# The last unit of the last cross-attention in a four-layer decoder gets its own PSUM layout

## The chip, the cores and the metric

The kernel runs on one core of a Trainium2 chip. The time is device microseconds of one launch, the median of three runs. Each profile is one execution, recorded by the hardware profiler, with its own time. Engines are written as in the profile: PE is TensorE's matmul, PEld its weight load, DVE VectorE, ACT ScalarE, POOL GpSimd, SP SyncE (which issues most DMAs). L263 means line 263 of the kernel.

## The reference, cut to what matters

A token stream x of 1024 positions and 128 channels passes four decoder layers, each with a self-attention, a cross-attention over a context of 6404 positions, and a feed-forward part. The change lies in the cross-attention of the last layer, which has 16 heads of 8 channels and a mask over the context:

```
q = _split_heads(Q @ Wq.T + bq)
k = _split_heads(K @ Wk.T + bk)
v = _split_heads(V @ Wv.T + bv)
scores = jnp.einsum('bhqd,bhkd->bhqk', q, k) / np.sqrt(D_HEAD).astype(np.float32)
scores = jnp.where(mask == 0, jnp.float32(-1000000000.0), scores)
attn = jax.nn.softmax(scores, axis=-1)
ctx = jnp.einsum('bhqk,bhkd->bhqd', attn, v)
...
return ctx @ Wo.T + bo
```

After it comes the last feed-forward part, a mixture of eight experts, and then the result is written.

## The kernel before, in words

**Tiling.** `l3_xattn` handles the 16 heads in four groups `g` of four heads, and the 1024 queries in two halves `h` of 512. One combination is a unit, `n = 2 * g + h`, so there are eight. In a unit, `pairs_core` loops over the context in 51 tiles of 128 keys (the last one has 4). The rows of two heads lie together in one tile of 128 partitions, 64 rows per head: the query and the key are split into bf16 parts stacked along these rows, and further rows carry the mask and the negative of each query's maximum. A matmul over the 64 rows thus gives scores that already have the maximum taken off, and the exponential needs nothing else. Such a two-head tile is called a pair; a unit has two pairs, `kP[0]`, `kP[1]` and `qP[0]`, `qP[1]`.

**One key tile of a unit.** For each of the four heads there is one score matmul (128 keys by 512 queries, one PSUM bank), one exponential from PSUM to SBUF, and one matmul with the values. The values have nine columns, the ninth all ones, so the sum of the exponentials comes with the result. The four heads' results go to four strips of 32 partitions in one bank, `acc`. The values of a tile are issued after the scores of the next tile (the list `late`), so that the PE need not wait for exponentials just started.

**Two forms of the loop.** `pairs_core` has two forms, chosen by whether the caller passes a list of work to do beside it:

```
        wide = beside is None
        matmul = nc.tensor.matmul if wide else self.matmul
...
                if wide:
                    both = ps.tile([P, 2, BANK], F32, tag="s", name="s")
                    p2 = pool.tile([P, 2, BANK], F32, tag="p", name="p", bufs=5)
...
                else:
                    ss = [ps.tile([P, BANK], F32, tag="s", name="s") for _ in range(2)]
                    pp = [pool.tile([P, BANK], F32, tag="p", name="p", bufs=10) for _ in range(2)]
...
                if wide:
                    nc.scalar.activation(p2[:n], both[:n], func)
                else:
                    for j in range(2):
                        nc.scalar.activation(pp[j][:n, :w], ss[j][:n, :w], func)
```

In the wide form a pair's scores lie in two neighbouring banks and one activation covers both heads (L1353); the matmuls show as L1348 (scores) and L1327 (values). In the narrow form each head has its own bank and activation (L1356), and all matmuls go through the helper at L263, which keeps them in the order of the program. The second layer's cross-attention, `l2_xattn`, uses the wide form in all eight units, with a sigmoid, 48 rows and eight value columns; its PSUM layout is one bank `m`, three pairs of banks `s` and one bank `acc`.

**What stands beside the units.** Each unit of `l3_xattn` but the last does the maxima of the next unit beside its own loop: `maxima(n + 1)` gives `pairs_max`, whose score matmuls go to pairs of banks `m2`, and VectorE reduces them (L1284). At its end `pairs_neg` negates the maxima, splits them into three bf16 parts in `mpad`, transposes them on the PE (L1304), and adds them into the next unit's `qP` on VectorE (L1306, once per pair). The last unit gets an empty tuple, so nothing stands beside it, but it is still the narrow form. The PSUM of all eight units is two `m2` pairs (four banks), three banks `s` and one bank `acc`.

**After the loop.** VectorE or ScalarE, by turns, copies `acc` to SBUF as `oT` (L269, L271). `pairs_norm` transposes it on the PE (L1377), takes the reciprocal of the sums (L1380) and writes the scaled result into `o` (L1382). After the eighth unit VectorE adds the value bias (L1725), and the output projection and the experts follow.

**Order.** Each engine has one queue that it works through in order. A scheduler puts the instructions in the queues by data and buffer dependences; a tile waits until the earlier user of its buffer is through, and a new pool's tile until earlier users of the same memory are.

Of the kernel before, what the change touches and what calls it, by code (L numbers as in the profile page):

```python
# [10 lines left out]
F32 = mybir.dt.float32  # L11
# [3 lines left out]
AF = mybir.ActivationFunctionType  # L15
ALU = mybir.AluOpType
AX = mybir.AxisListType
PSUM = bass.MemoryType.PSUM

P = 128  # L20
# [5 lines left out]
BANK = 512  # L26
# [188 lines left out]
class Decoder:  # L215
# [1156 lines left out]
    def pairs_norm(self, ps, pool, oT, o, g, h):  # L1372

        nc = self.nc
        m = ps.tile([P, 2, BANK], F32, tag="m2", name="m2")[:, 0, :]
        for i in range(4):
            nc.tensor.transpose(m[:, i * P:(i + 1) * P], oT[:, i * P:(i + 1) * P], self.ident)  # L1377
        mv = m.rearrange("p (t j r) -> p t j r", t=4, r=32)
        rd = pool.tile([P, 4, 4], F32, tag="rd", name="rd")
        nc.vector.reciprocal(rd, mv[:, :, :, 8])  # L1380
        ov = o[:, 4 * h:4 * h + 4, 32 * g:32 * g + 32].rearrange("p t (j r) -> p t j r", r=8)
        nc.vector.tensor_tensor(ov, mv[:, :, :, 0:8], rd[:, :, :, None].to_broadcast([P, 4, 4, 8]), ALU.mult)  # L1382
# [290 lines left out]
    def l3_xattn(self):  # L1673
        nc, tc = self.nc, self.tc
        w, some, kd = self.w3, self.some, self.kd3
        wo, bq = w[:, 384:512], w[:, 512:513]
        bv, bo = w[:, 514:642], w[:, 642:770]
        qd = self.dram.tile([P, 8, S], BF16, name="qd3")
        with tc.tile_pool(name="x", bufs=2) as pool:
            v = pool.tile([P, NKT, 16, 9], F32, tag="v", name="v", bufs=1)  # L1680
            nc.gpsimd.memset(v[:, :, :, 8:9], 1.0)
            mpad = pool.tile([P, 2, 4, P], F32, tag="mpad", name="mpad", bufs=1)
            nc.gpsimd.memset(mpad, 0.0)
            o = pool.tile([P, NT, D], F32, tag="o", name="o", bufs=1)
            kPs = [self.kP0, [pool.tile([P, NK], BF16, tag=f"kP{k}", name="kP", bufs=1) for k in range(2)]]
            qPs = [[pool.tile([P, S], BF16, tag=f"qP{i}{k}", name="qP", bufs=1) for k in range(2)] for i in range(4)]
            with tc.tile_pool(name="x0", bufs=2) as pool0, tc.tile_pool(name="x0_ps", bufs=2, space=PSUM) as ps0:
                ps = _Psum(ps0, m=2, m2=3)
                for i, src in ((6, some[:, 1:2]), (7, self.eps[:, 2:3])):
                    f = pool0.tile([P, BANK], BF16, tag="bar", name="fill")  # L1690
                    nc.vector.tensor_copy(f, src.to_broadcast([P, BANK]))
                    for h in range(2):
                        nc.sync.dma_start(out=qd[:, i, h * BANK:(h + 1) * BANK], in_=f)
                self.layernorm(ps)
                self.add_bias(bo)
                for _, hs, m in self.hidden(ps, [w[:, :128]], [self.xT]):
                    q = pool0.tile([P, BANK], F32, tag="k", name="q")
                    nc.vector.tensor_scalar(q, m, bq, some[:, 0:1], ALU.add, ALU.mult)
                    self.split(pool0, q, qd, self.QPART, hs.start, hs.stop)
                for g in range(4):  # L1700
                    self.pairs_read(qPs[g], qd, g, S)
                self.pairs_read(kPs[1], kd, 1, NK)
                vs = self.all_values(ps, v, w[:, 256:384], nc.scalar.copy)
                for step in self.pairs_max(ps, pool0, qPs[0], kPs[0], 0, mpad):
                    step(0)
                    step(1)
                    next(vs, None)
            with tc.tile_pool(name="x1", bufs=2) as pool1, tc.tile_pool(name="x1_ps", bufs=2, space=PSUM) as ps0:
                ps = _Psum(ps0, m2=2, s=3, acc=1)

                def maxima(n):
                    if n < 8:
                        return self.pairs_max(ps, pool1, qPs[n // 2], kPs[n // 2 % 2], n % 2, mpad)
                    return ()

                for n in range(8):
                    g, h = n // 2, n % 2
                    oT = pool1.tile([P, BANK], F32, tag="oT", name="oT")
                    self.pairs_core(ps, pool1, qPs[g], kPs[g % 2], v, g, h, oT, AF.Exp, 64, maxima(n + 1))
                    if h == 1 and g < 2:  # L1720
                        self.pairs_read(kPs[g], kd, g + 2, NK)
                    self.pairs_norm(ps, pool1, oT, o, g, h)
            with tc.tile_pool(name="x2", bufs=2) as pool2, tc.tile_pool(name="x2_ps", bufs=2, space=PSUM) as ps0:

                nc.vector.tensor_tensor(o, o, bv[:, None, :].to_broadcast([P, NT, D]), ALU.add)  # L1725
                self.small_out(_Psum(ps0, m=8), pool2, o, wo)
        self.held.close()
# [92 lines left out]
```

## Time and profile before

| | us |
|---|---|
| median of 3 runs | 6397.46 (6395.14 to 6400.81) |
| profiled execution, its own time | 6402.34 |
| its span, first to last instruction | 6400.5 |
| PE busy | 5934.1 (93%) |
| DVE busy | 3537.8 (55%) |
| ACT busy | 2987.7 (47%) |
| POOL busy | 2230.2 (35%) |

The units of the last cross-attention lie between about 5185 and 6207 us of the span. The last one begins with its first score matmul at 6086.04 and ends with the copy of `oT` at 6207.12; the experts end with the span at 6400.5. In the stretch from 6082 to 6207 the PE is busy for 100.16 us, ACT for 105.15, DVE for 2.77 and POOL not at all; DMA is near zero.

A row of instructions in time gives start, length, engine, line, operation, output and inputs, shape and how many were merged; in brackets stand the idle time before it and what ended that. A row of a group gives busy time and mean duration, and after the bar the idle time of its engine before these instructions. Durations of neighbours overlap in a pipeline, so the step from start to start is shorter than a duration.

### The profile page before, as it was taken

To read this page: it belongs to the slowest core of one execution; us is meant where nothing else is said; L and a number is where in the kernel's file an instruction comes from. 1 tells how busy PE (TensorE), PEld (TensorE's weight loads), DVE (VectorE), ACT (ScalarE), POOL (GpSimd) and SP (SyncE) were. 2 spreads that over 40 slices of the span, in tenths; PEclk is the share of its full clock that TensorE was granted. 3 is DMA by queue.
4 is the path that set the end of the run, shared out by engine and by line. 5 is a ranking of instruction groups with operands and counts; after the bars stand their busy time and mean duration, and the time that the engine had idled before them with its cause. 6 is when DMAs were issued, how large, how long until landed. Compare 5 with 4: busy or idle time off the path is not lost. (4 is left out here: it accounts for less than half of the span.)

```text
span 6400.5 us, 78103 instructions
## 1 busy us (share of the span) xinstructions
PE 5934.1 (93%) x30090; PEld 2158.5 (34%) x30090; DVE 3537.8 (55%) x6777; ACT 2987.7 (47%) x4024; POOL 2230.2 (35%) x1074
## 2 busy tenths in 40 slices
PE   6799999999999999999899968999988679999979
PEld 2233333434343434333375432111133211211126
DVE  5476666666666666664235461100025799999913
ACT  2323333343433333334311226999920058888872
POOL 1036667677676667678331530100001000000000
PEclk7799999999999999999989978999998679999999
DMA  3000000000000000000000013200023100000000
GB/s 102 4 1 1 1 1 1 1 1 1 1 1 1 1 1 1 1 6 7 31 2 14 0 67 92 66 16 1 1 80 103 52 1 21 1 21 1 1 6 29
DMA packets 65196, 118.23 MB, mean 18 GB/s; under 512 B 10510, under 2 KB 46630, under 8 KB 62774
## 3 DMA queue, kind: packets, MB, share of 16 engines
q1 hardware_dynamic: 64246, 109.95, 5.4%
q8 instruction: 236, 3.87, 0.2%
q10 hardware_dynamic: 576, 3.28, 0.2%
q14 instruction: 138, 1.13, 0.1%
HBM read 81.74 MB, written 31.41 MB: 18 GB/s over the span
## 5 line engine op out<-in xcount | busy, mean ns | idle before, releaser
L759 POOL TENSOR_TENSOR tot<-tot,p 128x1024 f32<-128x1024 f32 (+1 forms) x800 | 1885.2, 2357 | 668.4 <-ACT p L751 635.3
L678 DVE CUSTOM_DVE_ANT_0 junk<-m,bars 128x512 f32<-128x512 f32 (+1 forms) x1664 | 1114.4, 670 | 617.9 <-PE m L675 489.9
L751 ACT ACTIVATE p<-s,drop,keep 128x1024 f32<-128x1024 f32 (+1 forms) x416 | 500.7, 1204 | 1489.3 <-PE s L744 1475.7
L1284 DVE TENSOR_REDUCE mx<-m 128x2 f32<-128x1024 f32 (+4 forms) x928 | 1026.9, 1157 | 91.0 <-PE m L263 80.3
L1356 ACT ACTIVATE p<-s 128x512 f32<-128x512 f32 (+3 forms) x1824 | 924.7, 591 | 266.7 <-PE s L263 266.0
L675 PE MATMUL m<-kT,qT 64*128 64x512 f32 (+1 forms) x3328 | 940.9, 607 | 1.2 <-DVE mx L678 0.8
L739 PE MATMUL s<-qT,kT 64*128 64x512 f32 (+1 forms) x3264 | 832.5, 599 | 9.5 <-DVE p L749 9.5
L726 PE MATMUL acc<-p,v 128*64 128x512 f32 (+1 forms) x3264 | 791.2, 605 | 0.8 <-ACT p L751 0.7
L1353 ACT ACTIVATE p<-s 128x1024 f32<-128x1024 f32 (+1 forms) x816 | 750.9, 1179 | 27.3 <-PE s L1348 27.3
L749 DVE TENSOR_TENSOR p<-s,every 128x1024 f32<-128x1024 f32 x400 | 489.8, 1224 | 196.6 <-PE s L739 113.1
L1327 PE MATMUL acc<-p,v 128*8 128x512 f32 (+1 forms) x3264 | 552.4, 598 | 0.0
L751 ACT ACTIVATE p<-p,drop,keep 128x1024 f32<-128x1024 f32 x400 | 492.5, 1231 | 44.4 <-DVE p L749 44.0
L263 PE MATMUL m<-kP,qP 64*128 64x512 bf16 (+4 forms) x1856 | 374.0, 399 | 118.1 <-DVE mx L1284 57.5
L263 PE MATMUL acc<-p,v 128*9 128x512 f32 (+3 forms) x3648 | 471.5, 589 | 0.0
L739 PEld LDWEIGHTS s<-qT,kT 64*128 64x128 f32 (+1 forms) x3264 | 332.8, 187 | 395.7 <-issue 340.9
L675 PEld LDWEIGHTS m<-kT,qT 64*128 64x128 f32 x3328 | 305.5, 186 | 475.2 <-DVE mx L678 227.3
L263 PE MATMUL s<-qP,kP 64*128 64x512 bf16 (+3 forms) x1824 | 431.8, 385 | 33.2 <-ACT p L1356 29.8
L726 PEld LDWEIGHTS acc<-p,v 128*64 128x64 f32 (+1 forms) x3264 | 197.0, 136 | 530.3 <-issue 527.4
L1348 PE MATMUL s<-qP,kP 48*128 48x512 bf16 (+1 forms) x1632 | 250.9, 386 | 1.6 <-ACT p L1353 1.6
L269 DVE COPY oT<-acc 128x512 f32<-128x512 f32 x16 | 11.0, 689 | 431.6 <-PE acc L1327 301.8
L263 PEld LDWEIGHTS <-qP 64*128 64x128 bf16 x1856 | 122.9, 96 | 337.0 <-issue 263.4
L263 PEld LDWEIGHTS <-kP 64*128 64x128 bf16 x1824 | 94.1, 94 | 398.0 <-issue 390.0
(454 smaller groups left out, 4954.8 us busy)
## 6 DMA issues: line engine op xcount, KB each, us to landing
kd<-part SPq DMA_DIRECT2D x156, 128.0 KB
wb<-expert_weights SPq DMA_DIRECT2D x30, 512.0 KB
kP<-kd SPq DMA_DIRECT2D x24, 512.0 KB
kP<-kd SPq DMA_DIRECT2D x48, 192.0 KB
w_expert<-in_Y_w SPq DMA_DIRECT2D x8, 768.0 KB
qd<-part SPq DMA_DIRECT2D x36, 128.0 KB
qP<-qd SPq DMA_DIRECT2D x16, 256.0 KB
w_decay<-in_c_decay SPq DMA_DIRECT2D x4, 1024.0 KB
```

The lines of the kernel that those rows point to most:

```text
L263: return self.tc.keep_in_program_order(self.nc.tensor.matmul(*a, **k))
L675: nc.tensor.matmul(m[:, :b - a], lhsT=qT[r, q0:q0 + P], rhs=kT[r, a:b], start=True, stop=True)
L678: nc.vector.tensor_tensor_reduce(junk[:, :b - a], m[:, :b - a], bars[:, a:b], 1.0, -3.0e38, ALU.add, ALU.max, mx[:, t, j, c:c + 1])
L726: nc.tensor.matmul(acc[64 * j:64 * j + 64, :], lhsT=v[:n, t, 64 * j:64 * j + 64], rhs=pr[:n, j, :], start=t == 0, stop=t == NKT - 1, tile_ ...
L739: nc.tensor.matmul(s[:n, j, :], lhsT=kT[r, t * P:t * P + n], rhs=qT[r, hs], start=True, stop=t > t0)
L749: nc.vector.tensor_tensor(pr[:n], s[:n], every[:n], ALU.add)
L751: nc.scalar.activation(pr[:n], s[:n], AF.Exp, bias=drop[:n, t:t + 1], scale=keep[:n, t:t + 1])
L759: nc.gpsimd.tensor_tensor(tot[:n], tot[:n], pr[:n], ALU.add)
L1284: nc.vector.tensor_reduce(mx[:, t, 2 * pair:2 * pair + 2, c:c + 1], m[:, :, :b - a], AX.X, ALU.max)
L1327: matmul(acc[32 * j:32 * j + v.shape[3], off:], lhsT=v[:n, t, 4 * g + j, :], rhs=ws[j][:n, :BANK - off], start=t == 0, stop=t == nkt - 1, ...
L1353: nc.scalar.activation(p2[:n], both[:n], func)
L1356: nc.scalar.activation(pp[j][:n, :w], ss[j][:n, :w], func)
```

## The change: one more block for the last unit

The loop over units now ends after the seventh. The eighth runs in pools of its own, with the PSUM layout of the second layer's cross-attention: one bank `m`, three pairs of banks `s`, one bank `acc`. It is called without a list of work beside it, so that `pairs_core` takes the wide form. `pairs_norm` takes a bank `m` where the pool has no `m2`.

```diff
     def pairs_norm(self, ps, pool, oT, o, g, h):
 
         nc = self.nc
-        m = ps.tile([P, 2, BANK], F32, tag="m2", name="m2")[:, 0, :]
+        m = ps.tile([P, 2, BANK], F32, tag="m2", name="m2")[:, 0, :] if "m2" in ps.bufs else self.m(ps)
         for i in range(4):
             nc.tensor.transpose(m[:, i * P:(i + 1) * P], oT[:, i * P:(i + 1) * P], self.ident)
...
-                for n in range(8):
+                for n in range(7):
                     g, h = n // 2, n % 2
                     oT = pool1.tile([P, BANK], F32, tag="oT", name="oT")
                     self.pairs_core(ps, pool1, qPs[g], kPs[g % 2], v, g, h, oT, AF.Exp, 64, maxima(n + 1))
                     if h == 1 and g < 2:
                         self.pairs_read(kPs[g], kd, g + 2, NK)
                     self.pairs_norm(ps, pool1, oT, o, g, h)
+
+            with tc.tile_pool(name="x3", bufs=2) as pool1, tc.tile_pool(name="x3_ps", bufs=2, space=PSUM) as ps0:
+                ps = _Psum(ps0, m=1, s=3, acc=1)
+                oT = pool1.tile([P, BANK], F32, tag="oT", name="oT")
+                self.pairs_core(ps, pool1, qPs[3], kPs[1], v, 3, 1, oT, AF.Exp, 64)
+                self.pairs_norm(ps, pool1, oT, o, 3, 1)
             with tc.tile_pool(name="x2", bufs=2) as pool2, tc.tile_pool(name="x2_ps", bufs=2, space=PSUM) as ps0:
```

## The prediction

> **What bounds the kernel now.** I read the order of instructions in time around the last unit first, since only that unit is edited; then its groups with their idle time; then the same loop in the second layer's cross-attention, which already has the layout that the unit gets; then the granted clock in narrow stretches.
>
> One key tile of the last unit in the kernel before, in order of time (start, us, engine, line, operation):
>
> ```profile
> 6132.98 0.60 PE L263 MATMUL s<-qP,kP 64*128 64x512 bf16 x3
> 6133.41 2.06 ACT L1356 ACTIVATE p<-s 128x512 f32<-128x512 f32 x4 [0.29 <-PE s L263]
> 6134.06 0.37 PE L263 MATMUL s<-qP,kP 64*128 64x512 bf16 x1 [0.47 <-ACT p L1356]
> 6134.36 0.12 PEld L263 LDWEIGHTS acc<-p,v 128*9 128x9 f32 x8 [1.09 <-issue]
> 6134.36 1.05 PE L263 MATMUL acc<-p,v 128*9 128x512 f32 x8
> ```
>
> Three score banks are filled, the fourth score matmul waits until ScalarE has read the first of them, the values of the tile before (`acc`) are queued behind that fourth matmul on the in-order TensorE, and the next tile's scores are queued behind the values. So ScalarE runs dry once per tile: 0.29 us. Two such ACT rows start 2.353 us apart (6133.41 to 6135.76, 6138.12). Groups of the same stretch (6082 to 6206), busy and mean, then the idle time before:
>
> ```profile
> L1356 ACT ACTIVATE p<-s 128x512 f32<-128x512 f32 x200 | 103.1, 604 | 20.8 <-PE s L263 20.8
> L263 PE MATMUL acc<-p,v 128*9 128x512 f32 x400 | 52.3, 595 | 0.0
> L263 PE MATMUL s<-qP,kP 64*128 64x512 bf16 x200 | 49.7, 383 | 23.3 <-ACT p L1356 22.5 <-DVE qP L1306 0.2
> ```
>
> Each engine waits for the other: 20.8 us on ScalarE, 23.3 us on TensorE. VectorE, busy in all earlier units with the maxima of the next unit, has none to take here, and the stages after wait for this unit, so its length is path. Now the same loop in pairs of banks, one period in the second layer's cross-attention (48 rows and a sigmoid in place of 64 rows and an exponential):
>
> ```profile
> 4240.98 0.60 PE L1348 MATMUL s<-qP,kP 48*128 48x512 bf16 x4
> 4241.51 0.10 PEld L1327 LDWEIGHTS acc<-p,v 128*8 128x8 f32 x4 [0.42 <-issue]
> 4241.51 1.36 PE L1327 MATMUL acc<-p,v 128*8 128x512 f32 x8
> 4241.85 0.10 PEld L1327 LDWEIGHTS acc<-p,v 128*8 128x8 f32 x4 [0.23 <-ACT p L1353]
> 4242.81 0.11 PEld L1348 LDWEIGHTS <-kP 48*128 48x128 bf16 x4 [0.86 <-issue]
> ```
>
> The next period's scores are at 4242.81: 1.83 us. No score waits; the second half of the values waits 0.23 us for ScalarE, so ScalarE sets the pace. ScalarE's own rows, of that stage's last unit and of the start and end of the unit that is changed:
>
> ```profile
> 4585.55 93.36 ACT L1353 ACTIVATE p<-s 128x1024 f32<-128x1024 f32 x102
> ...
> 6086.74 4.03 ACT L1356 ACTIVATE p<-s 128x512 f32<-128x512 f32 x8 [6.94 <-PE s L263]
> ...
> 6203.99 2.02 ACT L1356 ACTIVATE p<-s 4x512 f32<-4x512 f32 x4 [0.27 <-PE s L263]
> ```
>
> 102 double-width activations in one piece with no idle time: 93.36 us. The same 51 key tiles take 119.27 us in the changed unit (6086.74 to 6203.99 + 2.02 = 6206.01).
>
> **The change, part by part.**
>
> *Width of the exponentials.* 204 of 512 become 102 of 1024. Step from one 512 to the next without a wait: (2.06 - 0.60) / 3 = 0.487 us. Of 1024: (93.36 - 1.0) / 101 = 0.914 us. A pair costs 0.974 now and 0.914 then: 102 x 0.060 = 6.1 us.
>
> *Layout.* Six banks of scores instead of three. In the new order of TensorE one more tile's scores stand in PSUM while ScalarE works, so the wait per tile goes: 2.353 - 4 x 0.487 = 0.405 us per tile (0.29 idle, the rest lost overlap), about 49 times 0.405 = 19.8 us (first two tiles already run without it). Sum of both: 25.9, and the end-to-end figures give the same: 119.27 - 93.36 = 25.9 us.
>
> The wide row is a sigmoid's. From both sides: 0.914 as in that row (gain 25.9), or no gain from the width at all, two narrow steps, 0.974 (99.4 us, gain 19.9). I take the row: the same line, shape, memory spaces and engine, and the narrow exponential and the wide sigmoid fit one line: 0.914 - 0.487 = 0.427 us for 512 more elements, which leaves 0.060 per instruction. [...]
>
> *Rows and columns.* 64 rows for 48 and 9 value columns for 8 change no time: 383 ns mean against 386 for scores, 595 against 604 for values. TensorE's work per tile is 0.53 for scores and 1.05 for values, 1.58 us, under 1.83.
>
> *The seam.* New pools open between units 7 and 8. In the built order TensorE's queue is the same there (mpad transposes, oT transposes, mpad transposes, eight scores, four values), but the first score now lies in banks of the last `m2` tile and waits for VectorE's second addition into qP. Before, it started at 6086.04; that addition ends at 6086.15 + 0.69 = 6086.84, so the score starts at 6086.89. Behind it on TensorE stand only this unit's scores. The first exponential then needs two matmuls: 0.49 us after the first score at full clock in the second layer (4105.33 to 4105.82), 0.60 at 4584.95 with ScalarE busy; I take 0.55, which gives 6087.44 instead of 6086.74: +0.7 us. `acc` is cleared after that addition instead of at 6080.85: 0.48 us on an idle VectorE, ended near 6087.4, a microsecond before the first values; uncovered it would be 0.48. No DMA and no other queue's order changes; SP's and GpSimd's lists are the same but for line numbers.
>
> *The norm.* One bank named `m` instead of half of `m2`; its transposes wait for the copy of `oT` as before. The last exponential to that copy was 1.11 us (6206.01 to 6207.12), and 1.12 in the second layer (4678.91 to 4680.03). Nothing.
>
> Sum: -25.9 + 0.7 = -25.2 us. The profiled execution was 6402.34 with a span of 6400.5; its span becomes 6375.3. It lies 4.9 above the median of the runs shown, all of which have the same unit, so the median goes from 6397.46 to **6372.3 us**.
>
> *What the shift meets.* After the unit come 193 us of output projection and experts, TensorE at work nearly throughout, with the clock at half in two stretches. Narrow stretches of the profile, the granted clock the number after POOL's:
>
> ```profile
> 6080.00:6085.00 5.00, 1.88 (x9) 1.58 (x9) 3.35 (x13) 0.00 (x0) 0.00 (x0) 0.53 0.00 0
> 6085.00:6090.00 5.00, 4.25 (x17) 1.42 (x20) 1.24 (x3) 3.26 (x7) 0.00 (x0) 0.79 0.02 3
> ...
> 6210.00:6215.00 5.00, 4.45 (x20) 4.21 (x21) 1.62 (x3) 1.87 (x2) 0.00 (x0) 0.50 0.02 1
> ...
> 6225.00:6230.00 5.00, 5.00 (x13) 3.05 (x12) 2.46 (x11) 0.60 (x1) 0.00 (x0) 0.50 0.34 118
> 6230.00:6235.00 5.00, 5.00 (x12) 2.10 (x12) 2.59 (x13) 4.25 (x6) 0.00 (x0) 0.95 0.10 39
> ```
>
> [...] I take 0 and put +-3 in the range. [...]
>
> **The rivals.**
>
> *The unit keeps a wait.* If three pairs are too few and ScalarE still loses its 0.29 us on every tile: 51 x 0.29 = 14.8 back, gain 10.4, 6387. For it: three pairs are still less than two tiles of scores. Against: the second layer's unit of 102 without a gap has the same three pairs.
>
> *The exponential is slower wide than the sigmoid.* Up to the upper bound, gain 19.2, 6378; nothing in the trace asks for it.
>
> [...]
>
> *No change.* The edit would have to miss the path. VectorE's idle 120 us before the copy of `oT` and the next stage's start right after it speak against; and the built kernel does contain 102 wide exponentials there.
>
> **How the numbers follow.** As worked out, with the tail's and seam's few microseconds: 0.86. Wide exponential slower or two clock windows lost (6378 to 6382): 0.05. A wait kept (about 6387): 0.04. No change: 0.02. Slower: 0.03. Likeliest 6372.3; its own range is -25.9 and 3 better in the tail, 6368.5, to 19.2 gained, 6378.3. The range for 8 in 10 is 6367.5 to 6379. What a measurement can tell from no change is 0.2%, 12.8 us, so faster is 0.86 + 0.05 and, where the kept wait is shorter, 0.01: 0.92; same 0.05 (the rest of the kept wait and no change); slower 0.03.
>
> **What would show it.** Right: the groups have L1353 of 102 (100 and two of 4 rows) between about 6087.4 and 6180.8 in one piece, idle time of it near zero; scores 1.83 us apart; the copy of `oT` at about 6182; the first wide score waiting for the addition into qP. Wrong: a row "PE s" with waits for ACT on every tile, starts 2 us or more apart, the exponentials' step above 0.95, or a clock under 1.00 in the middle of the unit. [...]

## The result

| | before | after |
|---|---|---|
| median, us | 6397.46 (7 executions, 6390.38 to 6425.81) | 6371.28 (7 executions, 6361.88 to 6381.14) |
| profiled execution, its own time | 6402.34 | 6379.08 |
| its span | 6400.5 | 6377.3 |
| second addition into qP ends, to copy of `oT` | 120.28 | 95.06 |
| exponentials of the unit, first start to last end | 119.27 | 93.41 |
| copy of `oT` to the end of the span | 193.38 | 193.19 |

The ratio of after to before is 0.9957, with a 95% interval of 0.994 to 0.9975: faster, by 26 us as the medians stand. The forecast was 6372.3, a difference of 25.2.

In the two profiles the difference of the spans is 23.2 us, and it can be split at the unit's edges. The stretch from the end of the second addition into qP to the copy of `oT` is 25.22 shorter; the tail after it is 0.19 shorter; and the changed kernel reached that addition 2.21 us later (6089.05 against 6086.84), in work that the change does not touch. 25.22 + 0.19 - 2.21 = 23.2. Executions of either kernel spread over 19 us and more, and the spread goes with the granted clock of the whole execution (in the rounds below the kernel before took 6379.13 us at a mean clock of 0.943 and 6425.13 at 0.933). The stretch from the addition to the copy repeats far better: 95.06 and 96.07 in two profiles of the change. The experiments below are therefore compared by this stretch, and by whole times only where there were rounds.

One key tile of the changed unit, in order of time (start, us, engine, line, operation):

```profile
6134.76 0.60 PE L1348 MATMUL s<-qP,kP 64*128 64x512 bf16 x4
6135.29 0.10 PEld L1327 LDWEIGHTS acc<-p,v 128*9 128x9 f32 x4 [0.42 <-issue]
6135.29 1.36 PE L1327 MATMUL acc<-p,v 128*9 128x512 f32 x8
6135.62 0.10 PEld L1327 LDWEIGHTS acc<-p,v 128*9 128x9 f32 x4 [0.23 <-ACT p L1353]
6136.59 0.11 PEld L1348 LDWEIGHTS <-kP 64*128 64x128 bf16 x4 [0.86 <-issue]
```

The next tile's scores start at 6136.59, 1.83 us on, where it was 2.353. The four scores run without a wait; what waits is the second half of the values, 0.23 us, for an exponential. The period is the second layer's to the hundredth, with 64 rows instead of 48 and an exponential instead of a sigmoid.

The groups of the changed stretch (6080 to 6185), busy and mean, then the idle time before:

```profile
L1353 ACT ACTIVATE p<-s 128x1024 f32<-128x1024 f32 x100 | 91.8, 1196 | 7.1 <-PE s L1348 7.1
L1327 PE MATMUL acc<-p,v 128*9 128x512 f32 x400 | 68.6, 595 | 0.0
L1348 PE MATMUL s<-qP,kP 64*128 64x512 bf16 x200 | 30.3, 381 | 1.5 <-DVE qP L1306 0.8 <-ACT p L1353 0.7
```

The 22.5 us that TensorE waited for ScalarE are gone but for 0.7. The 7.1 us that ScalarE still waits stand before the first exponential, where the maxima are finished. They stood there before, too, and are part of the 20.8 us in the group's row of the kernel before, as its waits show (total, times, longest):

```profile
ACT p L1356 <- PE s L263: 21.1, 50, 6.9
```

The longest wait, 6.9 us, is the one before the first exponential. So what is gone is the waits within the loop, about 14 us, and with them the overlap of neighbouring exponentials that each of them broke. ScalarE's own row of the changed unit:

```profile
6089.58 93.41 ACT L1353 ACTIVATE p<-s 128x1024 f32<-128x1024 f32 x102 [7.15 <-PE s L1348]
```

All 102 in one piece: a step of (93.41 - 1.0) / 101 = 0.915 us. The seam (the place where the seventh unit ends and the eighth begins), the engines together:

```profile
6088.36 0.69 DVE L1306 TENSOR_TENSOR qP<-qP,m 128x512 bf16<-128x512 bf16 x1 [0.46 <-PE m L1304]
6089.10 0.82 PE L1348 MATMUL s<-qP,kP 64*128 64x512 bf16 x6 [0.78 <-DVE qP L1306]
6089.30 0.48 DVE L1316 MEMSET acc<- 128x512 f32 x1 [0.25 <-DVE qP L1306]
```

The first score, which did not wait before, now waits 0.78 us for the second addition, as does the clearing of `acc`. The granted clock, the number after POOL's, at the seam and inside the unit:

```profile
6085.00:6090.00 5.00, 3.81 (x18) 2.69 (x19) 2.59 (x6) 0.42 (x1) 0.00 (x0) 0.66 0.00 0
...
6135.00:6140.00 5.00, 5.00 (x36) 0.86 (x32) 0.00 (x0) 5.00 (x7) 0.00 (x0) 1.00 0.00 0
```

In this execution the clock fell to half for one stretch of 3.4 us at the seam and was back at 6088.5, before the first score; inside the unit it is full. TensorE shows as busy for all of the 5 us there, as ScalarE does; which of them sets the pace is settled by the experiments.

### The profile page after: what moved, and what is told of

It is laid out like the page before. It is cut to its first block, busy times and chain, and to the rows that moved or that the text cites. A ratio compares the mean times of both kernels' runs of the same rounds, so it can differ in the third digit from the quotient of the medians.

```text
span 6377.3 us, 78098 instructions
## 1 busy us (share of the span) xinstructions
PE 5936.0 (93%) x30090; PEld 2163.1 (34%) x30090; DVE 3537.3 (55%) x6777; ACT 2975.8 (47%) x3922; POOL 2230.2 (35%) x1074
## 5 line engine op out<-in xcount | busy, mean ns | idle before, releaser
L1356 ACT ACTIVATE p<-s 128x512 f32<-128x512 f32 (+4 forms) x1620 | 819.3, 589 | 246.6 <-PE s L263 246.0
L1353 ACT ACTIVATE p<-s 128x1024 f32<-128x1024 f32 x918 | 844.3, 1181 | 34.4 <-PE s L1348 34.2
L1327 PE MATMUL acc<-p,v 128*8 128x512 f32 (+2 forms) x3672 | 622.6, 598 | 0.0
L263 PE MATMUL m<-kP,qP 64*128 64x512 bf16 (+4 forms) x1856 | 374.0, 399 | 115.6 <-DVE mx L1284 57.2
L263 PE MATMUL acc<-p,v 128*9 128x512 f32 (+2 forms) x3240 | 418.9, 589 | 0.0
L263 PE MATMUL s<-qP,kP 64*128 64x512 bf16 (+4 forms) x1620 | 382.3, 386 | 9.7 <-ACT p L1356 7.0
L1348 PE MATMUL s<-qP,kP 48*128 48x512 bf16 (+2 forms) x1836 | 281.8, 385 | 3.1 <-ACT p L1353 2.3
L263 PEld LDWEIGHTS <-qP 64*128 64x128 bf16 x1856 | 122.8, 96 | 334.3 <-issue 265.9
```

What stands on the lines that cost most here:

```text
L263: return self.tc.keep_in_program_order(self.nc.tensor.matmul(*a, **k))
L1327: matmul(acc[32 * j:32 * j + v.shape[3], off:], lhsT=v[:n, t, 4 * g + j, :], rhs=ws[j][:n, :BANK - off], start=t == 0, stop=t == nkt - 1, ...
L1348: matmul(ss[j][:n, :w], lhsT=kP[pair][r, t * P:t * P + n], rhs=qP[pair][r, hs], start=True, stop=not diag)
```

## The experiments

My theory: ScalarE sets the pace in the new unit. 19.8 us of the gain come from the banks (the fourth score no longer waits, and with it the values and the next tile's scores), 6.1 from the width, and the seam takes 0.7 back. The rivals: the gain comes from something else that the new block changes (the order of the matmuls, the pool, the form of the loop), or the size of it hangs on the clock that TensorE is granted. Edits are relative to the changed kernel and lie in the last unit alone.

### The pool without the layout

```diff
-                self.pairs_core(ps, pool1, qPs[3], kPs[1], v, 3, 1, oT, AF.Exp, 64)
+                self.pairs_core(ps, pool1, qPs[3], kPs[1], v, 3, 1, oT, AF.Exp, 64, ())
```

The empty list selects the narrow form, and `s=3` then means three single banks: the old loop, in the new pool.

> The last unit in pools of its own, but with three single banks and 512-wide exponentials as before: the pools are the whole change. My theory (width and layout are the gain, the pools cost a little): key tiles still 2.35 us apart, 204 exponentials in 119.3 us from the first to the end of the last, ScalarE idle about 20 us waiting for scores. The first score waits for VectorE's second addition into qP although it takes the same bank as before, because a new pool's first tile waits for all of the old pool: some 0.8 us later after the mpad transposes than before. Rival (the wait at the seam is for the banks of the last m2 tile, as I predicted): no wait here, since no score lies in m2's banks. Rival (something in the new pools themselves frees the loop): tiles under 2.2 us apart.

Measured: 6411.38 us (one execution). From the addition to the copy it took 6216.50 - 6083.93 = 132.6 us, where the old loop's 120.28 and the seam's 0.6 make 120.9. ScalarE and the first score:

```profile
6083.97 1.01 PE L263 MATMUL s<-qP,kP 64*128 64x512 bf16 x3 [0.78 <-DVE qP L1306]
6084.65 4.03 ACT L1356 ACTIVATE p<-s 128x512 f32<-128x512 f32 x8 [7.35 <-PE s L263]
6090.24 2.06 ACT L1356 ACTIVATE p<-s 128x512 f32<-128x512 f32 x4 [1.56 <-PE s L263]
6093.87 2.06 ACT L1356 ACTIVATE p<-s 128x512 f32<-128x512 f32 x4 [1.56 <-PE s L263]
...
6119.25 2.06 ACT L1356 ACTIVATE p<-s 128x512 f32<-128x512 f32 x4 [1.56 <-PE s L263]
6121.60 2.06 ACT L1356 ACTIVATE p<-s 128x512 f32<-128x512 f32 x4 [0.29 <-PE s L263]
```

Two things are seen. The wait of 0.78 us at the seam is there with the pool alone. And from the third tile on, nine tiles took 3.627 us each, ScalarE waiting 1.56 instead of 0.29; then the loop goes back to 2.353. (3.627 - 2.353) x 9 = 11.5 us, which is nearly all of the surplus of 11.7. The granted clock says why:

```profile
6080.00:6115.00 35.00, 31.88 (x114) 4.87 (x115) 2.48 (x6) 18.48 (x36) 0.00 (x0) 0.50 0.00 0
6120.00:6200.00 80.00, 64.05 (x409) 10.95 (x408) 0.00 (x0) 70.21 (x137) 0.00 (x0) 1.00 0.00 1
```

Half clock from 6078.75 to 6119.7, 41.0 us. TensorE shows as busy for 31.88 of 35 us in it. A clock that stays at half for long, the case for which I had given the changed kernel a chance of 0.03 to be slower, exists; in this run it hit the old loop.

### Six single banks, narrow

```diff
-                ps = _Psum(ps0, m=1, s=3, acc=1)
-                self.pairs_core(ps, pool1, qPs[3], kPs[1], v, 3, 1, oT, AF.Exp, 64)
+                ps = _Psum(ps0, m=1, s=6, acc=1)
+                self.pairs_core(ps, pool1, qPs[3], kPs[1], v, 3, 1, oT, AF.Exp, 64, ())
```

> Pools of its own, six single banks for scores, 512-wide exponentials: the layout without the width. My theory: ScalarE runs without gaps at 0.487 us an exponential, 1.95 us a key tile, 204 in about 99.5 us; so the layout alone is worth 19 to 20 us and the width the last 6. Rival (the width, with half as many instructions and handshakes, is what frees the loop): the tile stays near 2.35 us and the unit near 119 us.

Measured: 6373.99, and 101.28 us from the addition to the copy. ScalarE's row of the unit:

```profile
6077.71 99.64 ACT L1356 ACTIVATE p<-s 128x512 f32<-128x512 f32 x204 [7.14 <-PE s L263]
```

204 narrow exponentials in one piece. The banks alone are worth 119.27 - 99.64 = 19.6 us, and the width on top of them 99.64 - 93.41 = 6.2. The matmuls here are kept in the program's order by the helper at L263, as in the old loop, so their order is not where the gain comes from.

### Values on one tile only, wide and narrow

```diff
         def values(t, n, off, ws):
+            if few and t != nkt - 2:
+                return
...
-                       start=t == 0, stop=t == nkt - 1, tile_position=(0, 32 * j))
+                       start=few or t == 0, stop=few or t == nkt - 1, tile_position=(0, 32 * j))
```

With `few` set for the last unit this leaves out its matmuls with the values except for one tile; the output is then not the attention's. One kernel has it in the wide form with three pairs, one in the narrow form with three banks.

> The changed kernel with the value matmuls left out on 50 of the 51 key tiles of the last unit (its result there is not attention's). The profile has TensorE busy all of the time in this unit, so the question is what sets the pace. My theory (ScalarE): no change, 102 exponentials in 93.4 us, 1.83 us a tile. Rival (TensorE): a tile costs what the scores and the handshakes do, and the unit shortens clearly, to under 90 us.

> As the kernel with pools of its own, three single banks and 512-wide exponentials, and the value matmuls left out on 50 of the 51 key tiles. My theory (ScalarE ran dry because the next scores stand behind the values, and these behind the fourth score that waits for a bank): without the values in the queue the idle time goes, 1.95 to 2.0 us a tile and 100 to 102 us in all. Rival (three banks for four heads starve ScalarE by themselves, whatever is queued): the tile stays over 2.25 us.

Measured: 6364.5 and 6395.6 us. The second reached the unit 23.4 us later in its span than the first (second addition ended at 6097.98 against 6074.56), so the whole times don't compare. ScalarE's row of each, wide first:

```profile
6075.09 92.61 ACT L1355 ACTIVATE p<-s 128x1024 f32<-128x1024 f32 x102 [7.15 <-PE s L1350]
```

```profile
6098.70 99.84 ACT L1358 ACTIVATE p<-s 128x512 f32<-128x512 f32 x204 [7.35 <-PE s L263]
```

In the wide form, taking 400 value matmuls away from TensorE shortens the exponentials by 93.41 - 92.61 = 0.8 us: TensorE does not set the pace. In the narrow form the same removal takes 119.27 down to 99.84, what six banks gave with the values in place. So three banks are too few only because the values stand in TensorE's queue between the waiting fourth score and the next tile's first. The clock was at half through the whole unit in the narrow kernel and from 6077.4 on in the wide one. A stretch of each, wide first:

```profile
6080.00:6165.00 85.00, 56.56 (x186) 9.61 (x184) 0.00 (x0) 85.00 (x95) 0.00 (x0) 0.50 0.00 0
```

```profile
6100.00:6190.00 90.00, 90.00 (x184) 18.39 (x183) 0.00 (x0) 90.00 (x185) 0.00 (x0) 0.50 0.00 0
```

ScalarE is busy for all of the time in both: where it sets the pace and TensorE has room, half clock cost nothing.

### How many banks it takes

Four single banks in the narrow form (`s=4` and the empty list):

> Pools of its own, four single banks for scores, 512-wide exponentials. My theory: four banks, one for each head, already let ScalarE run without gaps, because the next tile's first three scores find their banks free while it works on the last: 1.95 to 2.0 us a tile, 99 to 102 us in all, as with six. Rival (more than one tile of scores must stand ahead): 2.1 us or more.

Two pairs, and then one pair, in the wide form, with the matmuls kept in the program's order:

```diff
-        matmul = nc.tensor.matmul if wide else self.matmul
+        matmul = nc.tensor.matmul if wide and ps.bufs["s"] == 3 else self.matmul
...
-                ps = _Psum(ps0, m=1, s=3, acc=1)
+                ps = _Psum(ps0, m=1, s=2, acc=1)
```

> Wide exponentials with two pairs of banks instead of three, matmuls kept in the program's order. My theory: worked out from the rows, the second pair's scores start when an exponential ends, then 1.05 to 1.36 us of values, then the next first pair: 1.84 to 1.95 us a tile, so 94 to 100 us for the 102. Rival (three pairs are what removes the wait): ScalarE idle by 0.3 us or more on each tile, 2.15 us a tile, 110 us or more.

> Wide exponentials with one pair of banks: the width without room. My theory: scores and exponentials take turns, about 1.2 us for an exponential to be through and 0.5 for two scores, 3.4 us a tile and 173 us in all, 50 us or more slower than before. Rival (the width carries the gain): not slower than before, 119 us or less.

| layout | time, one execution | addition to copy | exponentials | lost to half clock in these |
|---|---|---|---|---|
| 4 banks, narrow | 6371.96 | 102.56 | 100.93 | 0.92 |
| 6 banks, narrow | 6373.99 | 101.28 | 99.64 | 0 |
| 1 pair, wide | 6428.09 | 162.5 | 160.5 | 1.3 |
| 2 pairs, wide | 6380.75 | 99.64 | 97.77 | 1.02 |
| 3 pairs, wide (the change) | 6379.08 | 95.06 | 93.41 | 0 |

ScalarE's rows of the four banks:

```profile
6074.82 4.03 ACT L1356 ACTIVATE p<-s 128x512 f32<-128x512 f32 x8 [7.15 <-PE s L263]
6079.77 95.98 ACT L1356 ACTIVATE p<-s 128x512 f32<-128x512 f32 x196 [0.92 <-PE s L263]
```

The 0.92 lies at the third tile, while the clock was at half; without it the four banks take 100.0, and the fourth bank alone gives nearly all that six give. In the wide form two pairs are not quite enough: without the 1.02 they take 96.75, 3.3 us or 0.065 a tile more than three. (That kernel differs from the change in the order of its matmuls too, so the 3.3 us belong to both.) With one pair nothing overlaps between ScalarE and the scores; groups of that kernel from 6076 to 6221:

```profile
L1353 ACT ACTIVATE p<-s 128x1024 f32<-128x1024 f32 x93 | 95.2, 1024 | 51.4 <-PE s L263 51.4
L263 PE MATMUL s<-qP,kP 64*128 64x512 bf16 x184 | 36.3, 382 | 62.9 <-ACT p L1353 62.9
```

Each exponential waits 51.4 / 93 = 0.55 us for scores and takes 1.02, 1.57 together, and the unit is 42 us longer than before's. That is less than the 50 and more that I expected, since I had put an exponential that stands alone at 1.2 us. So the wide form by itself is no gain: it needs a second pair to be filled while the first is read.

### More work on ScalarE

```diff
                 ws += pp
...
+            ex = pool.tile([P, P], F32, tag="ex", name="ex")
+            nc.scalar.activation(ex[:n], ws[3][:n, :P], AF.Copy)
```

One more activation of 128 columns per key tile, into a tile that nothing reads.

> The changed kernel with one more activation per key tile on ScalarE (a copy of 128 columns within SBUF that nobody reads). My theory (ScalarE sets the pace): 0.060 + 128 x 0.00083 = 0.17 us more for each tile, 2.0 us a tile, 8.5 us more in all, near 102 us. Rival (TensorE sets the pace and the idle wait of 0.23 us for ScalarE in each tile is slack of TensorE's own making): less than 2 us more.

Measured: 6371.43, and 105.12 us from the addition to the copy, 10.06 more than the change. Three rows of ScalarE in the middle of the unit:

```profile
6150.06 2.39 ACT L1353 ACTIVATE p<-s 128x1024 f32<-128x1024 f32 x2
6151.88 0.77 ACT L1363 ACTIVATE ex<-p 128x128 f32<-128x128 f32 x1
6152.08 2.39 ACT L1353 ACTIVATE p<-s 128x1024 f32<-128x1024 f32 x2
```

Over the unit a tile takes 2.00 to 2.02 instead of 1.83, a little more than the 0.17 expected for the added work (0.060 + 128 x 0.427 / 512, an estimate from the steps of 0.487 and 0.914). That makes about 9.3 us in 51 tiles; one wait of 0.49 at half clock near the start and a first exponential that came 0.2 later make up the rest. The added work arrives whole at the end: ScalarE sets the pace.

### A colder seam

To see how easily each loop stays at half clock, 20 copies of 512 columns of qP onto themselves stand on VectorE ahead of the unit, which holds the first exponential back by some 3.5 us:

```diff
+                for i in range(20):
+                    nc.vector.tensor_copy(qPs[3][i % 2][:, BANK:], qPs[3][i % 2][:, BANK:])
                 self.pairs_core(ps, pool1, qPs[3], kPs[1], v, 3, 1, oT, AF.Exp, 64)
```

> As the run with pools of its own, three single banks and 512-wide exponentials, and 20 copies of qP onto itself on VectorE ahead of the unit, so that TensorE stands still for some microseconds and begins the unit at half clock. [...]

> The changed kernel with the same 20 copies of qP onto itself ahead of the last unit, so that it begins at half clock. [...]

Measured: 6417.62 narrow and 6381.59 wide. ScalarE's rows, narrow first:

```profile
6101.05 4.03 ACT L1356 ACTIVATE p<-s 128x512 f32<-128x512 f32 x8 [10.81 <-PE s L263]
6106.64 2.06 ACT L1356 ACTIVATE p<-s 128x512 f32<-128x512 f32 x4 [1.56 <-PE s L263]
6108.99 2.07 ACT L1356 ACTIVATE p<-s 128x512 f32<-128x512 f32 x4 [0.29 <-PE s L263]
```

```profile
6089.50 3.79 ACT L1353 ACTIVATE p<-s 128x1024 f32<-128x1024 f32 x4 [10.81 <-PE s L1348]
6093.97 1.94 ACT L1353 ACTIVATE p<-s 128x1024 f32<-128x1024 f32 x2 [0.69 <-PE s L1348]
6096.07 87.91 ACT L1353 ACTIVATE p<-s 128x1024 f32<-128x1024 f32 x96 [0.16 <-PE s L1348]
```

The theory that a longer pause would hold the narrow loop at half clock for long, and add 8 us or more to its exponentials, fell. Half clock lasted from 6099.7 to 6106.5, 6.8 us, one tile took the wait of 1.56, and the exponentials took 120.55 us, 1.28 more than before. The wide loop lost 0.69 + 0.16 us. In this one execution the pause was not what decides.

### Both in rounds

The pool alone once more, and the change itself, five rounds each, on the same chip:

> The kernel with pools of its own and the old loop again, timed in five rounds beside the kernel before, and one more profile. Theory: within 0.2% of before, 6390 to 6405, with single executions 10 to 25 us above that where the unit begins at half clock and stays there. Rival (the pools make the long stretch at half clock the rule): median 10 us or more above before.

> The changed kernel as it is, in five rounds beside the kernel before, and a second profile. Theory: median 25 us under before, 6365 to 6378; the profile has the 102 exponentials in 93.4 to 95 us, and no execution 10 us above the median. Rival (the gain of 25 us was in part the state of the clock in the one profile): exponentials in over 97 us, gain of the median under 19 us.

| | median, us | executions | range | ratio to before, 95% interval |
|---|---|---|---|---|
| before | 6401.62 | 21 | 6379.13 to 6425.13 | |
| pool alone | 6400.65 | 12 | 6385.59 to 6415.98 | 0.9997 (0.9983 to 1.0011) |
| the change | 6379.88 | 10 | 6359.95 to 6391.67 | 0.9958 (0.9941 to 0.9975) |

The new pool with the old loop is worth nothing that can be measured; the ratio of the change is that of the first measurement. (Had the 12 us that the profiles of the pool alone show been paid in all its executions and in none of the kernel before, its ratio would be 1.0019, outside the interval.)

Two expectations for the change failed. Its median was to lie between 6365 and 6378 and lies at 6379.88, 21.7 us under before's instead of 25; and no execution was to lie 10 us above the median, but one lies 11.8 above. The shortfall goes with the granted clock, whose mean was 0.939 in the median execution before and 0.938 in those about the median of the change. Executions with the same 0.938 took 6406.75 and 6407.38 us before and 6379.03 to 6379.99 with the change, 27 us apart. ScalarE's rows of the two profiled executions, pool alone first:

```profile
6091.98 2.06 ACT L1356 ACTIVATE p<-s 128x512 f32<-128x512 f32 x4 [1.56 <-PE s L263]
...
6121.00 2.06 ACT L1356 ACTIVATE p<-s 128x512 f32<-128x512 f32 x4 [1.57 <-PE s L263]
6123.36 2.06 ACT L1356 ACTIVATE p<-s 128x512 f32<-128x512 f32 x4 [0.29 <-PE s L263]
```

```profile
6089.32 3.77 ACT L1353 ACTIVATE p<-s 128x1024 f32<-128x1024 f32 x4 [7.38 <-DVE acc L1316]
6093.78 89.74 ACT L1353 ACTIVATE p<-s 128x1024 f32<-128x1024 f32 x98 [0.69 <-PE s L1348]
```

The pool alone again ran nine tiles at 3.627 us, at half clock for 40.9 us (6080.6 to 6121.5). The change, too, was at half clock over its start (6083.4 to 6093.65, 10.2 us), and lost 0.69 us by it; from the addition to the copy it took 96.07 us.

## Why the prediction was right, step by step

**The bound.** Right. The wait of the fourth score, with the values queued behind it, was the old loop's bound; taking the values away or adding a fourth bank removes it, each alone, down to two narrow steps per pair. One row was read too widely: the 20.8 us on ScalarE are not all waits of the loop, since 6.94 of them stand before the first exponential, and of TensorE's 23.3 us 22.5 are for ScalarE. The sum used neither figure; it rests on the period of 2.353 us.

**Width and layout.** 6.1 and 19.8 us were forecast, 6.2 and 19.6 measured, one by one. The choice at the disputed step was right: the row of the sigmoid gave 0.914 us, the exponential has 0.915. Narrow and wide steps, 0.488 in the six banks and 0.915, again leave about 0.06 per instruction beside 0.427 for 512 elements.

**The seam.** The size was right and the cause wrong. Forecast were a first exponential 0.60 us after the addition and +0.7 in all; measured are 0.53 after it, and since it began 0.10 before the end of the addition in the kernel before, +0.63. In the later profile of the change, which begins at half clock, the first exponential comes 0.74 after it. But the step that failed is "the first score now lies in banks of the last `m2` tile". In the changed kernel as built, the first score lies in bank 1 and the last two `m2` tiles in banks 4 to 7. In the run with the pool alone all scores lie in banks 1 to 3, and the wait is the same 0.78 us. In both, the first score and the clearing of `acc` wait for one and the same VectorE instruction, the second addition, which is the last VectorE work on a tile of the old pools; in the changed kernel so does the first exponential, whose output lies in SBUF and shares no bank with anything. So the wait comes with the new pool as a whole, not with a bank. That the clearing of `acc` came after the addition was covered, as forecast.

**The sum.** 119.27 - 93.41 = 25.86 for the exponentials, 0.63 back at the seam, 0.01 back between the last exponential and the copy (1.12 for 1.11): 25.22 against 25.2. In the later profile of the change, at half clock over its start, it was 24.2. That the medians of whole times came within 1 us of the forecast as well is in part luck: in the rounds they lie 21.7 apart.

**The norm and the tail.** 1.12 us to the copy as said. The tail moved by 0.19 us of the 3 allowed on each side. No run shows the 3 us, or the "two clock windows lost" that stand beside the 0.05. What the runs showed is a loss of 0 to 0.85 us over the start of the unit with three pairs. The tail is, over all 14 profiles here, 193.1 to 193.4 us where 17.1 us at half clock lie in the first 40 us after the copy of `oT`, as in the kernel before and in the first profile of the change, and 193.7 to 194.7 where more does. So the granted clock shows in it, by 0.3 to 1.6 us, and half the allowance would have done.

**The rivals.** No wait was kept with three pairs; with two (and the matmuls in the program's order) it would have been 0.065 us a tile, which is 3.3 and not the 14.8 that I gave it, and with one pair the change would have ended 42 us on the slow side. Half clock that stays on, which I gave the 0.03 for slower, is real, but in the narrow loop on three banks. There TensorE must wait for ScalarE and ScalarE for TensorE, so what TensorE loses goes into the period: its work per tile grows from the 1.58 us of the prediction to 2.85 (estimated from two rows of the second layer in the kernel before, 0.95 for the scores at 4110.05 and 1.90 for the values at 4108.22), by 1.27, and the period from 2.353 to 3.627, by 1.27. In the new loop it did not stay: in the four profiles of three pairs with all values the full clock was back within 6 us of the first exponential, and the loss was 0 to 0.85 us. That the old loop suffers from this in some executions of the kernel before is likely from the pool-alone runs, and would widen its spread; its one profile shows the clock back at 6087.05, so that it happens there is not shown, and no part of the 26 us is put down to it.

## What to carry to other kernels

Before adding buffers, look at what is queued on the in-order engine between the waiting producer and its next useful work: here a wait of one matmul for a bank cost 0.4 us per tile only because the value matmuls stood behind it, and one more bank was enough. Take the step of a wider instruction from a row of the same shape on the same engine and memory, even with another function: here the sigmoid's row gave 0.914 us and the exponential took 0.915. When one engine sets the pace with slack on the other, a loop is also insured against the other's clock, as far as the slack goes: with few values half clock cost nothing, with all values it cost 0.5 to 0.9 us over the start of the unit. Two engines that wait for each other have no such cover: the old loop on three banks lost 11.5 us to half clock in the pool alone.

## What the hardware showed that was not expected

**Half clock at a busy TensorE.** In two profiles of the pool alone TensorE stayed at half clock for 41.0 and 40.9 us while its matmul records fill 91% of the time (31.88 of 35 us in the first, 31.86 in the second). What brings the clock back is open. In these two profiles TensorE pauses 0.26 us in each tile of 3.627. In the first of them it has no pause from 6085.30 to 6089.66, 4.36 us, as these rows show, and the clock stayed at half for another 30 us:

```profile
6085.30 2.54 PE L263 MATMUL s<-qP,kP 64*128 64x512 bf16 x5 [0.32 <-ACT p L1356]
6087.77 1.89 PE L263 MATMUL acc<-p,v 128*9 128x512 f32 x8
```

Other runs agree. In the narrow kernel with few values the records fill all of 90 us (6100 to 6190) at half clock, with one score matmul per exponential. The other way round, in the kernel before the clock came back at 6087.05, 0.16 us after a pause of 0.24 us:

```profile
6086.89 2.83 PE L263 MATMUL s<-qP,kP 64*128 64x512 bf16 x6 [0.24 <-DVE qP L1306]
```

So gaps in the records don't decide it, and no run here separates the kinds of matmul.

**Full clock with a half-idle TensorE.** With one pair TensorE waited for ScalarE 62.9 of 145 us (6076 to 6221), and the clock was at half until 6078.56 and full for the rest. So records for little more than half of the time went with a full clock that stayed there, while 91% did not bring it back above. What keeps the full clock and what brings it back thus look like different things; no run here was made to test it.
